# Weight copies on GpSimd, a longer last chunk and fewer closing passes in the setup of a fused conv, attention and mixture kernel

## The chip, the core and the metric

The kernel runs on one core of a Trainium2 chip. A core has five engines with a queue each: TensorE (PE in the profile), VectorE (DVE), ScalarE (ACT), GpSimd (POOL) and SyncE (SP), which here issues the DMAs. The metric is the device time of one launch in microseconds (us). It is 2541.94 us for the kernel before, the median of three runs.

## The reference

x has 128 images of 128 channels and 16 x 16 positions. Layer 0 normalises x by groups of four channels (32 groups) within each image, and puts that through a convolution block; layer 1 (two selective state-space scans and a mixture of eight experts on layer-normed tokens) takes most of the time and isn't touched by the change. Cut to what matters:

```python
def _gn(v, G=32, eps=1e-5):
    g = v.reshape(B_, G, C_ // G, H_, W_)
    m = jnp.mean(g, axis=(2, 3, 4), keepdims=True)
    s = jnp.var(g, axis=(2, 3, 4), keepdims=True)
    return ((g - m) / jnp.sqrt(s + eps)).reshape(v.shape)

def _bn(x, gamma, beta):
    m = jnp.mean(x, axis=(0, 2, 3), keepdims=True)
    v = jnp.var(x, axis=(0, 2, 3), keepdims=True)
    xhat = (x - m) * jax.lax.rsqrt(v + EPS)
    return xhat * gamma[None, :, None, None] + beta[None, :, None, None]

h = _act_quant(_bn(x, gamma1, beta1))          # clip to 0..1, 15 levels
wq1 = _weight_quant(w1) * pat1[None, None, :, :]
out = _conv3x3(h, wq1)
out = _act_quant(_bn(out, gamma2, beta2))
wq2 = _weight_quant(w2) * pat2[None, None, :, :]
out = _conv3x3(out, wq2)
return out + x

x = x + _L0_conv_ref(_gn(x), ...)
```

The batch norm needs the statistics of all images before one value of h can be made. Here it and the group norm are folded into one scale and one bias for each channel and image.

## The kernel before

**Stages.** The setup (about the first 77 us) reads x into 64 tiles `xr` of two images each, channels on the 128 partitions, and makes from it the scale `sc1` and the bias `bi1` (128 x 128: channel by image). `conv1` then quantises image pairs into padded tiles `hpad` and convolves them, with bfloat16 weights `wq1`; `conv2` follows, and then layer 1, whose steps stand in an order written out by hand.

**Statistics in chunks.** The images are cut in three chunks, `cuts = [0, 48, 112, 128]` for 128 images. VectorE takes the statistics of an image with `bn_stats` (L469). In the first two chunks every fourth image (b % 4 == 3, `by_scalar`) is ScalarE's instead: a pass that sums it (L464), a GpSimd pass over one column, `neg`, which makes the negative mean of it (L465), and a pass that sums the squares around that mean (L453). The square of an image stands behind the sum of the next one in ScalarE's queue, so one image lies between a `neg` and its use.

After a chunk's images its means and variances are made in 13 passes (L480 to L498), which stand on GpSimd for the first two chunks and on VectorE for the last; two of them go through TensorE, which averages over the four channels of a group (`gm_ps` L494, `gv_ps` L500), and ScalarE copies the one (L495) and takes the square root of the other (L502). VectorE takes the reciprocal (L472), and `normed` improves it by one Newton step and scales means and variances with it (L435 to L445), again on GpSimd for the first two chunks and on VectorE for the last. The reciprocal of the middle chunk is issued when the loop is at the last but one image:

```python
if b in (cuts[1] + 30, B - 2):
    with tc.issue_after(last.ins):
        nc.vector.reciprocal(ga[:, cuts[c - 1] : cuts[c]], ga[:, cuts[c - 1] : cuts[c]])
    normed(c - 1)
```

A scheduler puts the instructions of each engine into one queue, which is worked off in order; in VectorE's queue this reciprocal stands ahead of the statistics of image 127, and those ahead of the last chunk's passes.

**Closing the norm.** Over the 128 images VectorE makes the batch mean `bm` (L519, L520) and variance `bv` (L521 to L526), and GpSimd closes with six passes (L528 to L533): rs = (bv + EPS) ** -0.5, times 15 gamma (`g15`), sc1 = ga rs, bi1 = (shift - bm) rs + 15 beta (`b15`). A branch on the kind of the weights (L216 to L220) follows on every engine, and then `conv1`, which begins with ScalarE's passes over x with sc1 and bi1 (L547), like passes on GpSimd (L549), and VectorE's clipping into `hpad` (L183).

**Weights.** `conv_weights` quantises a convolution's weights (128 x 9 x 128 in float32), in steps that are set between the statistics. It makes three bfloat16 parts of them: the rounded weights (L160), the rounded rest (L174) and what is left after that (L176), with a subtraction on VectorE (L162) between the first two and one on GpSimd (L175) between the last two. The three copies are ScalarE's. It is called for w1 in the setup, and for w2 while `conv1` runs.

Of the kernel before, what the change touches and what calls it, by code (L numbers as in the profile page):

```python
# [11 lines left out]
ALU = mybir.AluOpType  # L12
# [4 lines left out]
EPS = 1e-5  # L17
# [17 lines left out]
def kernel(ctx: ExitStack, tc: tile.TileContext, a: dict):  # L35

    nc = tc.nc
    x_d, out_d = a["x"], a["out"]
    B = x_d.shape[0]
# [45 lines left out]
    mhalf = const.tile([P, 8], F32, name="mhalf")  # L85
# [25 lines left out]
    def row(name, ap):  # L111
        t = const.tile([P, ap.shape[0]], F32, name=name)
        nc.sync.dma_start(t, ap.partition_broadcast(P))
        return t
# [11 lines left out]

    CROSS, DIAGONAL = [1, 3, 4, 5, 7], [0, 2, 4, 6, 8]

    def conv_weights(parts, how, setup, psums, w, pat, taps, tag):


        def everywhere(n):

            mx_ps = psums.tile([P, P], F32, name=f"mx_ps_{tag}{n}", tag="mx_ps", bufs=1)
            nc.tensor.transpose(mx_ps, mx.to_broadcast([P, P]), ident)
            nc.vector.tensor_reduce(am, mx_ps, AX.X, ALU.max)

        t = setup.tile([P, 9, P], F32, name=f"t_{tag}", tag="t")
        nc.scalar.activation(t, w, AF.Tanh)
        yield  # L140
        mx = setup.tile([P, 1], F32, name=f"mx_{tag}", tag="mx")
        nc.vector.tensor_reduce(mx, t, AX.XY, ALU.max, apply_absolute_value=True)
        yield
        am = setup.tile([P, 1], F32, name=f"am_{tag}", tag="am")
        everywhere(0)
        yield
        nc.vector.tensor_scalar(am, am, 2.0, None, ALU.mult)
        rm = setup.tile([P, 1], F32, name=f"rm_{tag}", tag="rm")
        nc.vector.reciprocal(rm, am)
        nc.vector.tensor_scalar(t, t, rm, 0.5, ALU.mult, ALU.add)  # L150
        yield
        nc.vector.tensor_scalar(t, t, NLEV, MAGIC, ALU.mult, ALU.add)
        yield
        nc.vector.tensor_scalar(t, t, MAGIC, 2.0, ALU.subtract, ALU.mult)
        yield
        nc.vector.scalar_tensor_tensor(
            w, t, -NLEV, pat.unsqueeze(2).to_broadcast([P, 9, P]), ALU.add, ALU.mult
        )
        yield
        nc.scalar.copy(parts[:, :, 0, :], w)  # L160
        yield
        nc.vector.tensor_tensor(t, w, parts[:, :, 0, :], ALU.subtract)  # L162
        yield

        nc.vector.tensor_reduce(mx, t, AX.XY, ALU.max, apply_absolute_value=True)
        yield
        everywhere(1)
        yield
        nc.vector.tensor_scalar(am, am, 0.0, 2.0, ALU.not_equal, ALU.mult)
        for tap in range(9):  # L170
            if tap not in taps:
                nc.vector.scalar_tensor_tensor(am, pat[:, tap : tap + 1], 0.0, am, ALU.not_equal, ALU.max)
        nc.vector.tensor_copy(how, am)
        nc.scalar.copy(parts[:, :, 1, :], t)  # L174
        nc.gpsimd.tensor_tensor(w, t, parts[:, :, 1, :], ALU.subtract)  # L175
        nc.scalar.copy(parts[:, :, 2, :], w)  # L176

    def quantise(q, hp, nq):

# [64 lines left out]
    how1 = const.tile([P, 1], mybir.dt.int32, name="how1")  # L244
    how2 = const.tile([P, 1], mybir.dt.int32, name="how2")
    pat1, pat2 = row("pat1", a["L0_conv_pat1"]), row("pat2", a["L0_conv_pat2"])
# [90 lines left out]
    with tc.tile_pool(name="w1p", bufs=1) as w1p:  # L337

        sc1 = w1p.tile([P, B], F32, name="sc1")
        bi1 = w1p.tile([P, B], F32, name="bi1")  # L340
        wq1 = w1p.tile([P, 9, 3, P], BF16, name="wq1")
        o1st = res.tile([P, NP, 6], F32, name="o1st")
        with tc.tile_pool(name="setup1", bufs=1) as setup, tc.tile_pool(
# [45 lines left out]
            made = next(tables)  # L389
            w1 = w1p.tile([P, 9, P], F32, name="w1", tag="w")  # L390
            nc.sync.dma_start(w1, a["L0_conv_w1"])
            weights = conv_weights(wq1, how1, w1p, psa, w1, pat1, CROSS, "c1")
            with tc.issue_after(made.ins):
                next(weights)
            for _ in range(2):
# [15 lines left out]
            def tb(name):  # L411
                return setup.tile([P, B], F32, name=name)

            mean, var, dm, gm, dev, qv, ga, neg, shift = (
                tb(n) for n in ("mean", "var", "dm", "gm", "dev", "qv", "ga", "neg", "shift")
            )
            cuts = [0, 3 * B // 8, 7 * B // 8, B]
            half_ = setup.tile([P, B], F32, name="half_")
            b15 = setup.tile([P, 1], F32, name="b15")
            nc.vector.tensor_scalar(b15, bet1, NLEV, None, ALU.mult)  # L420
            g15 = setup.tile([P, 1], F32, name="g15")
# [96 lines left out]
            bm = setup.tile([P, 1], F32, name="bm")  # L518
# [4 lines left out]
            nc.vector.tensor_tensor(var, var, dev, ALU.add)  # L523
            bv = setup.tile([P, 1], F32, name="bv")
            nc.vector.tensor_reduce(bv, var, AX.X, ALU.add)
            nc.vector.tensor_scalar(bv, bv, 1.0 / B, None, ALU.mult)  # L526
            rs = setup.tile([P, 1], F32, name="rs")
            nc.gpsimd.tensor_scalar(rs, bv, EPS, None, ALU.add)  # L528
            nc.gpsimd.tensor_tensor(rs, rs, mhalf[:, 0:1], ALU.pow)
            nc.gpsimd.tensor_tensor(rs, rs, g15, ALU.mult)  # L530
            nc.gpsimd.tensor_scalar(sc1, ga, rs, None, ALU.mult)
            nc.gpsimd.tensor_scalar(bi1, shift, bm, rs, ALU.subtract, ALU.mult)
            nc.gpsimd.tensor_scalar(bi1, bi1, b15, None, ALU.add)  # L533


        def conv1(taps, nq):
            with tc.tile_pool(name="pb", bufs=3) as pb, tc.tile_pool(
                name="psb", bufs=4, space=PSUM
            ) as psb:
                weights = conv_weights(wq2, how2, w1p, psb, w2, pat2, DIAGONAL, "c2")  # L540

                def quantised(i):
# [659 lines left out]
    def part_f(i):  # L1202
# [84 lines left out]
    parts = {  # L1287
        "a": part_a, "c": part_c, "x": part_x, "bc": part_bc, "sx": part_sx, "z": part_z, "xt": part_xt, "g": part_g,
        "s": part_s, "b": part_b, "m": part_m, "y": part_y, "n": part_n, "r": part_r, "o": part_o, "e": part_e, "p": part_p,
        "f": part_f,  # L1290
    }
# [42 lines left out]
```

## Time and profile before

| | us |
|---|---|
| median of 3 runs (2541.1 to 2543.05) | 2541.94 |
| the profiled execution | 2543.71 |
| its span | 2542.0 |
| first matmul of the first convolution, into the span | 77.40 |
| VectorE busy, 57.50 to 64.60 | 0.00 |
| GpSimd busy, 57.50 to 64.60 | 4.46 |
| ScalarE busy, 57.50 to 64.60 | 2.90 |

The page of a profile has the busy time of each engine, and then the span in 40 slices of which each has one digit, the busy share in tenths. A line of a timeline has: start in the span, length (both us), engine, line of the kernel, operation, out<-in by the program's names, shapes as partitions x elements with the type, how often, and in square brackets how long the engine was idle before and what ended that. A line of the waits has: engine, what waited and its line, what it waited for and its line, then us in total, times, longest us.

### The profile page before, as it was taken

To read this page: it belongs to the slowest core of one execution; us is meant where nothing else is said; L and a number is where in the kernel's file an instruction comes from. 1 tells how busy PE (TensorE), PEld (TensorE's weight loads), DVE (VectorE), ACT (ScalarE), POOL (GpSimd) and SP (SyncE) were. 2 spreads that over 40 slices of the span, in tenths; PEclk is the share of its full clock that TensorE was granted. 3 is DMA by queue.
4 is the path that set the end of the run, shared out by engine and by line. 5 is a ranking of instruction groups with operands and counts; after the bars stand their busy time and mean duration, and the time that the engine had idled before them with its cause. 6 is when DMAs were issued, how large, how long until landed. Compare 5 with 4: busy or idle time off the path is not lost.

```text
span 2542.0 us, 49262 instructions
## 1 busy us (share of the span) xinstructions
PE 2412.9 (95%) x15936; PEld 1481.2 (58%) x15936; DVE 2239.5 (88%) x6094; ACT 2178.8 (86%) x4462; POOL 1639.8 (65%) x1733
## 2 busy tenths in 40 slices
PE   0888789999999999999999999999999999999997
PEld 0345456666666666666666666666666666666663
DVE  7886799999999999999999999999999999999883
ACT  7778699898889889888989888898988889898881
POOL 4677036666766666676666676666667666666676
PEclk9999899999999999999999999999999999999998
DMA  9368624444344444434434444443443444443333
GB/s 313 132 228 272 189 58 120 120 124 120 111 130 133 120 118 130 118 118 133 129 119 125 125 111 123 131 125 120 126 121 115 129 133 124 121 124 117 107 124 110
DMA packets 302166, 339.57 MB, mean 134 GB/s; under 512 B 56768, under 2 KB 226752, under 8 KB 301888
## 3 DMA queue, kind: packets, MB, share of 16 engines
q1 hardware_dynamic: 301888, 336.21, 43.4%
q8 instruction: 133, 2.18, 0.3%
q14 instruction: 145, 1.19, 0.2%
HBM read 262.72 MB, written 56.62 MB: 126 GB/s over the span
## 4 chain that ended last, share of the span: by engine, by line
PE 90%; DVE 3%; ACT 2%; issue 1%; DMA 1%; POOL 1%; SPq 0%; ACTq 0%; POOLq 0%; DVEq 0%
PE f_ps L1211 17%; PE x_ps L899 13%; PE y_ps L1034 10%; PE z_ps L942 9%; PE o_ps L1094 9%; PE sg L987 5%; PE xt_ps L954 4%; PE y_ps L1040 4%; PE g_ps L973 4%; PE cv L209 4%; PE n_ps L1067 1%; PE u_ps L1116 1%; PE f_ps L1206 1%; PE u_ps L772 1%; PE rt_ps L1123 1%; PE yt_ps L653 1%
## 5 line engine op out<-in xcount | busy, mean ns | idle before, releaser
L1199 POOL TENSOR_TENSOR gb<-gb,u2T 128x512 f32<-128x512 f32 x512 | 641.1, 1276 | 124.6 <-PE y_ps L1040 63.7
L917 DVE SCALAR_TENSOR_TENSOR xc<-x_ps,cw,xc 128x510 f32<-128x510 f32 (+2 forms) x768 | 570.9, 743 | 47.9 <-ACT xc L911 38.6
L1050 POOL TENSOR_TENSOR yg<-yg,z 128x512 f32<-128x512 f32 x256 | 325.8, 1278 | 349.1 <-DVE yg L1046 154.9
L1211 PE MATMUL f_ps<-gb,ew 128*128 128x512 f32 x1024 | 509.0, 601 | 7.2 <-POOL gb L1199 6.9
L899 PE MATMUL x_ps<-uT,wx 128*128 128x512 f32 x768 | 400.7, 603 | 9.5 <-ACT e L753 3.3
L753 ACT ACTIVATE e<-sg 128x512 f32<-128x512 f32 x512 | 299.3, 591 | 49.9 <-PE sg L987 44.4
L753 ACT ACTIVATE e<-e,ends 128x128 f32<-128x128 f32 x1024 | 325.0, 392 | 0.0
L1034 PE MATMUL y_ps<-e,xt 128*64 128x256 f32 x2048 | 317.7, 389 | 0.2 <-DVE yg L1046 0.2
L1015 DVE TENSOR_TENSOR e<-e,g_ps 128x1024 f32<-128x1024 f32 x256 | 311.2, 1216 | 5.6 <-ACT e L753 2.6
L917 DVE SCALAR_TENSOR_TENSOR bc<-x_ps,cw,bc 128x510 f32<-128x510 f32 (+2 forms) x384 | 286.5, 746 | 20.6 <-ACT bc L911 4.5
L1211 PEld LDWEIGHTS f_ps<-gb,ew 128*128 128x128 f32 x1024 | 180.5, 192 | 173.7 <-issue 135.4
L942 PE MATMUL z_ps<-uT,wz 128*128 128x512 f32 x512 | 272.2, 613 | 1.4 <-issue 0.8
L911 ACT ACTIVATE xc<-x_ps,cb,cw 128x512 f32<-128x512 f32 x256 | 199.0, 777 | 64.0 <-PE x_ps L899 57.1
L1094 PE MATMUL o_ps<-wo,yg 128*128 128x128 f32 x2048 | 251.4, 276 | 0.2 <-DVE e L1020 0.2
L1094 PEld LDWEIGHTS o_ps<-wo,yg 128*128 128x128 f32 x2048 | 240.5, 193 | 11.1 <-DVE g L1171 8.4
L1046 DVE SCALAR_TENSOR_TENSOR yg<-xc,dcol,y_ps 128x512 f32<-128x512 f32 x256 | 189.4, 740 | 50.5 <-PE y_ps L1040 47.1
L1082 POOL TENSOR_TENSOR rr<-rr,mhalf 128x8 f32<-128x8 f32 x64 | 110.0, 1718 | 161.7 <-DVE g L1173 82.5
L1040 PE MATMUL y_ps<-e,xt 128*64 128x128 f32 x2048 | 199.0, 273 | 0.0
L987 PE MATMUL sg<-rows,cols 128*128 128x256 bf16 x1024 | 192.1, 274 | 5.8 <-ACT e L753 2.9
L1040 PEld LDWEIGHTS y_ps<-e,xt 128*64 128x64 f32 x2048 | 147.0, 137 | 74.1 <-DVE e L1020 0.5
L1034 PEld LDWEIGHTS y_ps<-e,xt 128*64 128x64 f32 x2048 | 118.9, 136 | 100.9 <-issue 53.8
L209 PE MATMUL cv<-hpad,wq 128*128 128x512 bf16 x640 | 162.3, 398 | 12.8 <-DVE hpad L183 12.7
(283 smaller groups left out, 4810.2 us busy)
## 6 DMA issues: line engine op xcount, KB each, us to landing
gb<-gd SPq DMA_DIRECT2D x256, 512.0 KB
e<-cum SPq DMA_DIRECT2D x256, 256.0 KB
xr<-in_x SPq DMA_DIRECT2D x64, 256.0 KB
cc<-bc SPq DMA_DIRECT2D x128, 128.0 KB
out<-ob SPq DMA_DIRECT2D x64, 256.0 KB
y<-yt SPq DMA_DIRECT2D x60, 256.0 KB
yt<-y SPq DMA_DIRECT2D x60, 256.0 KB
o<-o SPq DMA_DIRECT2D x56, 256.0 KB
```

Of the source, the lines that this page charges most:

```text
L753: nc.scalar.activation(out, in_, func, **more)
L899: nc.tensor.matmul(ps, wx[d][:, n * P : (n + 1) * P], uTs[i], start=True, stop=True)
L917: nc.vector.scalar_tensor_tensor(acc[:, :, to], raw[:, :, of], cw[:, d, n, 3 - back : 4 - back], acc[:, :, to], ALU.mult, ALU.add,)
L942: nc.tensor.matmul(ps, wz[:, d, n * P : (n + 1) * P], uTs[i], start=True, stop=True)
L987: nc.tensor.matmul(sg[:, :, of], c_[:, k, d, s, half, :], r_[:, :, d, s, of], start=True, stop=True)
L1015: nc.vector.tensor_tensor(e0.rearrange("p h t l -> p h (t l)"), e0.rearrange("p h t l -> p h (t l)"), gps[i, d, k][:, 0:NT].unsqueeze(1).t ...
L1034: nc.tensor.matmul(y_ps[64 * q : 64 * q + 64, k, :], xt[:, 2 * k + s0, 64 * h : 64 * h + 64], e0[:, h].rearrange("p t l -> p (t l)"), star ...
L1040: nc.tensor.matmul(y_ps[64 * q : 64 * q + 64, k, s1 * P : (s1 + 1) * P], xt[:, 2 * k + s1, 64 * h : 64 * h + 64], e1[:, h, :], start=False ...
L1050: large(nc.gpsimd.tensor_tensor(yg, yg, zs[i, d][:, n, :], ALU.mult))
L1094: nc.tensor.matmul(o_ps[:, (2 * j + d) * P : (2 * j + d + 1) * P], ygs[i, d, n][:, t * P : (t + 1) * P], wo[d][:, n, :], start=(n == 0), s ...
L1199: large(nc.gpsimd.tensor_tensor(gb[:, e], gb[:, e], u2Ts[i], ALU.mult))
L1211: nc.tensor.matmul(f_ps, ew[:, e, :], gbs[i, e], start=False, stop=(e == NE - 1))
```

## The change

Three edits, all in the setup. `conv_weights` takes the function that makes its three bfloat16 copies as an argument, and for w1 that is GpSimd's `tensor_copy`; for w2 the copies stay with ScalarE. The cuts become 48, 104 and 128, so that the middle chunk has 56 images and the last 24, and ScalarE's share ends with image 103. And EPS is added by VectorE in the instruction that divides the variance, and GpSimd's six closing passes become four: shift = (shift - bm) g15, rs = bv ** -0.5, bi1 = shift rs + b15, sc1 = ga rs g15.

```diff
-    def conv_weights(parts, how, setup, psums, w, pat, taps, tag):
+    def conv_weights(parts, how, setup, psums, w, pat, taps, tag, cast=nc.scalar.copy):
...
-        nc.scalar.copy(parts[:, :, 0, :], w)
+        cast(parts[:, :, 0, :], w)
...
-        nc.scalar.copy(parts[:, :, 1, :], t)
+        cast(parts[:, :, 1, :], t)
         nc.gpsimd.tensor_tensor(w, t, parts[:, :, 1, :], ALU.subtract)
-        nc.scalar.copy(parts[:, :, 2, :], w)
+        cast(parts[:, :, 2, :], w)
...
-            weights = conv_weights(wq1, how1, w1p, psa, w1, pat1, CROSS, "c1")
+            weights = conv_weights(wq1, how1, w1p, psa, w1, pat1, CROSS, "c1", cast=nc.gpsimd.tensor_copy)
...
-            cuts = [0, 3 * B // 8, 7 * B // 8, B]
+            cuts = [0, 3 * B // 8, 13 * B // 16, B]
...
-            nc.vector.tensor_scalar(bv, bv, 1.0 / B, None, ALU.mult)
+            nc.vector.tensor_scalar(bv, bv, 1.0 / B, EPS, ALU.mult, ALU.add)
             rs = setup.tile([P, 1], F32, name="rs")
-            nc.gpsimd.tensor_scalar(rs, bv, EPS, None, ALU.add)
-            nc.gpsimd.tensor_tensor(rs, rs, mhalf[:, 0:1], ALU.pow)
-            nc.gpsimd.tensor_tensor(rs, rs, g15, ALU.mult)
-            nc.gpsimd.tensor_scalar(sc1, ga, rs, None, ALU.mult)
-            nc.gpsimd.tensor_scalar(bi1, shift, bm, rs, ALU.subtract, ALU.mult)
-            nc.gpsimd.tensor_scalar(bi1, bi1, b15, None, ALU.add)
+            nc.gpsimd.tensor_scalar(shift, shift, bm, g15, ALU.subtract, ALU.mult)
+            nc.gpsimd.tensor_tensor(rs, bv, mhalf[:, 0:1], ALU.pow)
+            nc.gpsimd.tensor_scalar(bi1, shift, rs, b15, ALU.mult, ALU.add)
+            nc.gpsimd.tensor_scalar(sc1, ga, rs, g15, ALU.mult, ALU.mult)
```

## The prediction

> **What bounds the kernel now.** The page comes first. It says TensorE is the bound of the whole, and slice 2 of 40 says where it isn't:
>
> ```profile
> PE 2412.9 (95%) x15936; PEld 1481.2 (58%) x15936; DVE 2239.5 (88%) x6094; ACT 2178.8 (86%) x4462; POOL 1639.8 (65%) x1733
> PE   0888789999999999999999999999999999999997
> ```
>
> A slice is 63.6 us. In the first one PE does nothing: it is the setup, in which x comes in, its statistics are taken and the first norm is closed. Everything after it follows in a fixed order behind the first convolution, so the change is worth what it takes off the moment when that convolution starts, 77.40 us into the span. The waits of the stretch 57 to 76 us and VectorE's timeline say what ends last there:
>
> ```profile
> DVE ga L472 <- ACT ga L502: 7.2, 1, 7.2
> ACT q L547 <- POOL bi L533: 7.1, 1, 7.1
> ```
> ```profile
> 51.81 5.64 DVE L469 BATCH_NORM_STATS2 bst<-xr 128x6 f32<-128x256 f32 x15 [0.33 <-DMA xr<-in_x]
> 64.61 0.55 DVE L472 RECIPROCAL ga<-ga 128x64 f32<-128x64 f32 x1 [7.17 <-ACT ga L502]
> 65.49 0.18 DVE L483 TENSOR_TENSOR mean<-bst 128x16 f32<-128x16 f32 x1
> 76.03 0.16 DVE L202 TENSOR_SCALAR less<-less_ps 128x1 f32<-128x1 f32 x1 [3.75 <-issue]
> ```
>
> VectorE has taken the statistics of all but one image by 57.45 us, when the last of x has come, and then stands 7.17 us: the reciprocal of the middle chunk is ahead of the last image in its queue and waits for that chunk's square root on ScalarE. So the last chunk starts at 65.45 and not at 57.9. Why the middle chunk is late is in ScalarE's timeline:
>
> ```profile
> 29.79 1.15 ACT L160 CAST wq<-w 128x1152 bf16<-128x1152 f32 x1 [3.21 <-DVE w L156]
> 38.49 1.14 ACT L174 CAST wq<-t_c 128x1152 bf16<-128x1152 f32 x1
> 42.11 1.15 ACT L176 CAST wq<-w 128x1152 bf16<-128x1152 f32 x1 [0.84 <-POOL w L175]
> 59.56 0.51 ACT L453 ACTIVATE junk<-xr,neg 128x256 f32<-128x256 f32 x1
> 64.27 0.31 ACT L502 ACTIVATE ga<-gv_ps,epsc 128x64 f32<-128x64 f32 x1 [2.44 <-PE gv_ps L500]
> ```
>
> ScalarE takes every fourth image of the first 112 (a sum, L464, and a square, L453, 1.235 us a pair, no gap from 48.4 on) and ends at 60.17, long after image 111 has come. In front of it stand the three weight copies, with two waits of 3.21 and 0.84 us. GpSimd's timeline has what the change touches there:
>
> ```profile
> 32.32 1.50 POOL L483 TENSOR_TENSOR mean<-bst 128x48 f32<-128x48 f32 x1
> 39.72 2.36 POOL L175 TENSOR_TENSOR w<-t_c,wq 128x1152 f32<-128x1152 f32 x1 [2.51 <-ACT wq L174]
> 72.36 0.23 POOL L528 TENSOR_SCALAR rs<-bv 128x1 f32<-128x1 f32 x1 [1.26 <-DVE bv L526]
> 72.67 0.58 POOL L529 TENSOR_TENSOR rs<-rs,mhalf 128x1 f32<-128x1 f32 x1
> 73.33 0.19 POOL L530 TENSOR_TENSOR rs<-rs,g 128x1 f32<-128x1 f32 x1
> 73.63 0.61 POOL L531 TENSOR_SCALAR sc<-ga,rs 128x128 f32<-128x128 f32 x1
> 74.23 0.81 POOL L532 TENSOR_SCALAR bi<-shift,bm,rs 128x128 f32<-128x128 f32 x1
> 75.14 0.61 POOL L533 TENSOR_SCALAR bi<-bi,b 128x128 f32<-128x128 f32 x1
> ```
>
> The last six are in series between VectorE's variance (72.28) and ScalarE's first pass over x (75.79).
>
> **What the Trainium skill says.** "Perfetto Trace Analysis", section "Tensor Engine Instruction": ScalarE, VectorE and GpSimd are strict FIFO. The trace agrees: ScalarE stood 3.21 us before L160 with image 47 landed. So a copy moved to GpSimd holds up what is queued behind it there. "SBUF — State Buffer", section "Who interferes with whom": a VectorE instruction with two SBUF inputs and a GpSimd instruction that reads SBUF exclude each other, whoever comes second waits for the other's end. The trace agrees: L483 on GpSimd took 1.50 us, against 0.38 for the wider one of the next chunk, and ended 0.19 us after VectorE's two-input L162 (32.29 to 33.63); VectorE's L172 over one column, issued at 40.33, ended at 42.10 with GpSimd's L175.
>
> **Part 1, copies on GpSimd.** No GpSimd copy stands in the trace of before. From below: the memset of 648 bfloat16 takes 0.637 us, so 0.83 ns a column and about 0.1 start, 1.06 us for 1152. The skill ("GPSIMD Engine Reference", section "4.1 Engine selection") calls one-input operations roughly line-rate, at 1.2 GHz an estimate of 0.96 and a 0.2 start, 1.16 us; no run here shows it. Between: the two-scalar pass of L549 takes 0.555 us for 256 columns where nothing disturbs it and the like pass L444 0.203 for 16, so 1.47 ns a column, 1.9 us for 1152. From above: the one-operation passes (0.614 for 128 columns, 0.214 for one) cost 3.15 ns a column, 3.8 us. I take 1.2, since a copy computes nothing.
>
> The order of the built program shows where they stand. ScalarE only loses the three copies and two images. On GpSimd the first copy is before neg of image 47, the second before L175, the third between neg of 59 and of 63, and the eight first passes of the first chunk's Newton step now stand before neg of 79. Behind a copy waits neg (L465), and for it ScalarE's square. With the durations above:
> - first copy 29.83 (w is ready at 29.75) to 31.03, neg of 47 to 31.26, then the 13 passes L480 to L498. They took 31.72 to 36.84 with 1.3 us of the lock in it; it stays, since L162 still comes at 32.29: 31.26 to 36.24.
> - neg of 51 and 55 to 36.70, second copy to 37.90, L175 (2.36) to 40.32, neg of 59 to 40.55: ScalarE's square of 59 at 40.61 instead of 43.17.
> - third copy to 41.75, neg of 63 to 41.98, its square at 42.04 instead of 44.40.
> - then 1.235 us an image, but the square of 79 waits for the Newton step (44.74 to 47.31) and comes at 47.60. Six pairs on, the square of 103 ends at 55.07.
>
> That is 60.17 - 55.07 = 5.1 us, of which the two images are 2.47. A tenth more for a copy costs 0.3 us, since three stand in series.
>
> **Part 2, chunks of 48, 56 and 24.** Beside the two images: the 13 passes over 56 columns instead of 64 save 0.03 us each, 0.4 us, so the last chunk starts 5.5 us earlier, at 59.95. That is still after x's last image, at 57.45, so VectorE's two more statistics (0.34 us each, by 57.9) are hidden; 2 us are left before the DMA is the bound. VectorE's 20-odd passes over 24 columns instead of 16 cost 0.009 us each (0.17 at 16, 0.29 at 128), +0.2 us. The middle chunk's Newton step on GpSimd starts from the same reciprocal as before and so keeps its distance of 3 us from VectorE's sum L519.
>
> **Part 3, four closing passes.** L528 and L530 go, EPS rides on L526 for nothing. After the variance: 0.08 wait, 0.58 power, 0.1, then bi1 (multiply and add, as L549, 0.39 for 128 columns), 0.1, then sc1 (two products, between L531's 0.61 and L532's 0.81: 0.7), 0.04: 2.0 us instead of 3.51, 1.5 less. But two things eat it. VectorE comes back from the branch at 76.03, 3.75 us after its variance whatever GpSimd does, and the first padded image, which ScalarE let start at 76.91, could then start at 76.1 at best: 0.8 of the 1.5. And the pass over shift (0.81, as L532) now runs on GpSimd from the moment L445 has ended (71.09 in before's times), held behind L522 to 71.37, so to 72.2; VectorE's two-input L523, due at 71.48, must wait for it, +0.7. Sum of the tail with the 24 columns: -0.8 + 0.7 + 0.2 = +0.1. If L523 doesn't wait and ScalarE's earlier start counts in full, it is -1.3.
>
> **Sum.** -5.5 + 0.1 = -5.4 us. The profiled execution took 2543.71 us, its span and 1.71 around it, so 2538.3 by its own time; it lies 1.77 above the median of 2541.94, and by the median the forecast is 2536.5. Later stages I let move as a block: SP's queue isn't altered, its weight loads are issued by 83.3 us and the first store of o1 would come at about 86; w2, issued at 53.8, is used at about 79.
>
> **Rivals.** 0.2% is 5.1 us here, about what a measurement of this kernel can tell from no change.
> - The tail pays: 5.5 + 1.3 = 6.8, 2535.1. For it: the lock needs L528 to start in a gap of 0.1 us. Against: L172 and L483 show that it bites.
> - The copies run at the pace of the q passes (1.9 us): the same steps give 62.0 for the last chunk, 3.4 us gained, 2538.6 with the tail. For it: that pass is the nearest one-input row over a long tile. Against: it computes, a copy doesn't.
> - Slower: GpSimd's queue takes ScalarE's place as the bound, at the third copy and L465 behind it. At 3.8 us a copy the same steps put the square of 63 some 4.5 us later than before and the last chunk at 67.8: 2.4 us lost, 2544.4. It decides from 3.0 us a copy, where the last chunk starts at 65.4. For it: the one-operation passes do run that slowly. Against: those are arithmetic passes.
> - The gain is lost later, 2542: something after the first convolution's start would have to wait for what hasn't moved. Against: PE is busy for 77.6 of the 80.4 us that follow 77.40, and the transfers of that stage end early.
>
> **Chances.** Forecast 0.50 (0.37 of it beyond 5.1 us, as it lies on the line), tail pays 0.20, q pace 0.20 (0.02 beyond), slower 0.06 (half of it beyond 5.1 us the other way, if a copy is slower still), lost later 0.04. So faster 0.59, slower 0.03, same 0.38. The range goes from the tail's case with copies of 1.06 us and 0.9 us of scatter (2533.8) to copies of 2.4 us, whose last chunk starts at 63.6 (2540.3); it leaves out the slower and lost cases.
>
> **What would show it.** Copies on GpSimd of 1.2 us; ScalarE's last square near 55; VectorE's reciprocal L472 near 59; L523 held until the shift pass ends; the first convolution's first matmul near 72. It is wrong if a copy takes 2 us or more, or if the first matmul moves and the end doesn't.

## The result, and the profile after

| | before | after |
|---|---|---|
| median, us (11 runs each) | 2543.05 (2540.63 to 2548.52) | 2536.57 (2534.36 to 2538.47) |
| ratio, 95% interval | | 0.9973 [0.9963, 0.9982] |
| the profiled execution | 2543.71 | 2536.24 |
| its span | 2542.0 | 2534.5 |

The changed kernel is 6.5 us faster by the medians (4.6 to 9.4 by the interval); 5.4 were forecast. That the forecast of 2536.5 lies so near the median of 2536.57 is partly luck, since the kernel before ran 1.1 us longer beside it than in the three runs that the forecast started from. The comparison that counts is 5.4 against 6.5, and it has to be made stage by stage.

The page of the changed kernel, its busy times and TensorE's row of the 40 slices:

```profile
PE 2415.3 (95%) x15936; PEld 1480.5 (58%) x15936; DVE 2241.5 (88%) x6096; ACT 2174.2 (86%) x4451; POOL 1641.9 (65%) x1732
PE   0889889999999999999999999999999999999997
```

TensorE is busy for 2.4 us longer than before and the kernel is shorter nevertheless: what went is idle time, 6.3 us of it ahead of the first convolution, which the digits are too coarse to show. The waits of the stretch 50 to 76 us show it:

```profile
ACT q L545 <- POOL sc L531: 5.4, 1, 5.4
...
DVE less L202 <- issue: 3.7, 1, 3.7
...
DVE ga L472 <- ACT ga L502: 1.4, 1, 1.4
```

VectorE's wait for the middle chunk's square root was 7.2 us and is 1.4. VectorE's timeline of the changed kernel, the lines that answer to those of before:

```profile
58.85 0.50 DVE L472 RECIPROCAL ga<-ga 128x56 f32<-128x56 f32 x1 [1.40 <-ACT ga L502]
59.67 0.20 DVE L483 TENSOR_TENSOR mean<-bst 128x24 f32<-128x24 f32 x1
...
65.97 0.35 DVE L523 TENSOR_TENSOR var<-var,dev 128x128 f32<-128x128 f32 x1
...
66.68 0.15 DVE L526 TENSOR_SCALAR bv<-bv 128x1 f32<-128x1 f32 x1
70.54 0.16 DVE L202 TENSOR_SCALAR less<-less_ps 128x1 f32<-128x1 f32 x1 [3.70 <-issue]
70.61 0.76 DVE L183 TENSOR_SCALAR hpad<-q 128x512 uint8<-128x512 f32 x2
```

The last chunk starts at 59.67, before at 65.49. The variance is ready at 66.83, VectorE is back from the branch at 70.54, and the first padded image follows at once; before, it stood 0.73 us more until ScalarE had made its input. GpSimd's timeline of the changed kernel has the three copies and the four closing passes:

```profile
29.82 1.14 POOL L160 CAST wq<-w 128x1152 bf16<-128x1152 f32 x1 [3.57 <-DVE w L156]
...
36.59 1.14 POOL L174 CAST wq<-t_c 128x1152 bf16<-128x1152 f32 x1
...
40.31 1.14 POOL L176 CAST wq<-w 128x1152 bf16<-128x1152 f32 x1
...
65.70 0.85 POOL L528 TENSOR_SCALAR shift<-shift,bm,g 128x128 f32<-128x128 f32 x1
66.92 0.58 POOL L529 TENSOR_TENSOR rs<-bv,mhalf 128x1 f32<-128x1 f32 x1 [0.37 <-DVE bv L526]
67.61 0.45 POOL L530 TENSOR_SCALAR bi<-shift,rs,b 128x128 f32<-128x128 f32 x1
68.04 0.45 POOL L531 TENSOR_SCALAR sc<-ga,rs,g 128x128 f32<-128x128 f32 x1
```

And ScalarE's timeline of the changed kernel: the square of image 59, the last square (image 103), and the middle chunk's root.

```profile
40.39 0.51 ACT L453 ACTIVATE junk<-xr,neg 128x256 f32<-128x256 f32 x1 [0.59 <-POOL neg L465]
...
53.99 0.51 ACT L453 ACTIVATE junk<-xr,neg 128x256 f32<-128x256 f32 x1
...
58.51 0.31 ACT L502 ACTIVATE ga<-gv_ps,epsc 128x56 f32<-128x56 f32 x1 [2.34 <-PE gv_ps L500]
```

The square of 59 waits 0.59 us behind the second copy and the subtraction on GpSimd, which is what the copies cost there, and the last square starts at 53.99 instead of 59.56.

How far the gain reaches, as starts in us into the span; the marks are those that the runs below are compared by:

| | before | after | gain |
|---|---|---|---|
| last chunk's first pass (L483) | 65.49 | 59.67 | 5.82 |
| variance (L526) | 72.13 | 66.68 | 5.45 |
| first padded image (L183) | 76.91 | 70.61 | 6.30 |
| first matmul of the first convolution | 77.40 | 71.09 | 6.31 |
| first matmul of the second convolution | 164.56 | 158.95 | 5.61 |
| first `dt_ps` matmul of layer 1 | 280.76 | 275.04 | 5.72 |

So 5.8 us come at the last chunk, the tail adds 0.5, the first convolution gives 0.7 back, and layer 1 starts 5.7 us earlier. The remaining 1.8 of the span's 7.5 appear inside layer 1, where two executions of one kernel can differ by more (last lines of the section on the first convolution).

### The profile page after: what moved, and what is told of

Same layout as the page of the kernel before. It is cut to its first block, busy times and chain, and to the rows that moved or that the text cites. A ratio compares the mean times of both kernels' runs of the same rounds, so it can differ in the third digit from the quotient of the medians.

```text
span 2534.5 us, 49248 instructions
## 1 busy us (share of the span) xinstructions
PE 2415.3 (95%) x15936; PEld 1480.5 (58%) x15936; DVE 2241.5 (88%) x6096; ACT 2174.2 (86%) x4451; POOL 1641.9 (65%) x1732
## 4 chain that ended last, share of the span: by engine, by line
PE 89%; DVE 4%; DMA 3%; ACT 2%; POOL 1%; issue 1%; SPq 0%; DVEq 0%; POOLq 0%; ACTq 0%
PE f_ps L1209 17%; PE x_ps L897 13%; PE y_ps L1032 10%; PE z_ps L940 9%; PE o_ps L1092 9%; PE sg L985 5%; PE xt_ps L952 4%; PE y_ps L1038 4%; PE g_ps L971 4%; PE cv L209 4%; DMA xr<-in_x 2%; PE n_ps L1065 1%; PE f_ps L1204 1%; PE u_ps L1114 1%; PE u_ps L770 1%
## 5 line engine op out<-in xcount | busy, mean ns | idle before, releaser
L1032 PEld LDWEIGHTS y_ps<-e,xt 128*64 128x64 f32 x2048 | 118.9, 136 | 101.0 <-issue 54.0
```

Source lines behind the costliest of these rows:

```text
L1032: nc.tensor.matmul(y_ps[64 * q : 64 * q + 64, k, :], xt[:, 2 * k + s0, 64 * h : 64 * h + 64], e0[:, h].rearrange("p t l -> p (t l)"), star ...
```

## The experiments

The theory was that of the prediction: parts 1 and 2 both shorten ScalarE's queue and so the wait at L472, and the tail is worth little because VectorE comes back from the branch late. The rivals were its own (the tail counts in full, copies at the q passes' pace, GpSimd's queue is the new bound, the gain is lost later), and one more: one part alone carries the gain. Every run is compared with the kernel before on its own chip; the medians of different rows come from several chips, so the ratios and the starts are to be compared, not the medians.

| run | last chunk | first matmul | second conv. | median, us | ratio [95%] |
|---|---|---|---|---|---|
| e1_copies | 62.36 | 74.31 | 162.40 | 2540.71 | 0.9985 [0.9978, 0.9992] |
| e2_cut | 62.82 | 75.05 | 163.14 | 2542.45 | 0.9994 [0.9985, 1.0002] |
| e3_closing | 65.50 | 76.48 | 164.25 | 2543.74 | 0.9997 [0.9989, 1.0005] |
| e4_twice | 60.58 | 72.08 | 159.55 | 2539.15 | 0.9980 [0.9971, 0.9989] |
| e5_cut96 | 58.01 | 69.62 | 157.54 | 2537.32 | 0.9970 [0.9959, 0.9980] |
| e6_sc_twice | 59.61 | 70.73 | 159.15 | 2539.11 | 0.9979 [0.9973, 0.9986] |
| e7_scalar_var | 60.19 | 71.27 | 158.39 | 2538.01 | 0.9975 [0.9966, 0.9983] |
| e9_mult | 65.48 | 76.92 | 164.05 | 2542.86 | 0.9997 [0.9989, 1.0006] |
| e9_muladd | 59.73 | 71.25 | 159.06 | 2536.41, one run | |
| e8_warm | 59.63 | 71.07 | 157.56 | 2535.61 | 0.9971 [0.9962, 0.9980] |
| e10_best | 58.19 | 69.60 | 156.74 | 2535.14 | 0.9965 [0.9951, 0.9978] |
| e11_again | 59.69 | 70.86 | 158.88 | 2540.13, one run | |

### One part at a time

Each of the first three is the changed kernel with two of its three parts undone. What the first undoes is the cut and the closing:

```diff
-            cuts = [0, 3 * B // 8, 13 * B // 16, B]
+            cuts = [0, 3 * B // 8, 7 * B // 8, B]
...
-            nc.gpsimd.tensor_scalar(shift, shift, bm, g15, ALU.subtract, ALU.mult)
...
+            nc.gpsimd.tensor_scalar(rs, bv, EPS, None, ALU.add)
```

> Only the copies go to GpSimd; cuts and closing passes are those of the kernel before. Queue theory (the last chunk waits for GpSimd's and ScalarE's queues, and every edit acts through them): with copies of 1.14 us, as measured in the changed kernel, the steps of the prediction put ScalarE's last square at 57.4 us instead of 60.2 and the last chunk's first pass at 62.7 instead of 65.5; first matmul of the first convolution 2.8 us earlier than before, at 74.6. Rival (GpSimd gives back what ScalarE is spared, since the squares wait for the one-column passes behind the copies, and the whole gain is the cut's): last chunk at 65.5 and no gain.

The second undoes the copies (and the closing, as above), so that the cut stands alone:

```diff
-            weights = conv_weights(wq1, how1, w1p, psa, w1, pat1, CROSS, "c1", cast=nc.gpsimd.tensor_copy)
+            weights = conv_weights(wq1, how1, w1p, psa, w1, pat1, CROSS, "c1")
```

> Only the cuts change (48, 104, 128). Queue theory: two images fewer on ScalarE, 2.47 us, last square at 57.7, last chunk's first pass at 63.0; the longer last chunk gives back 0.2, first matmul about 2.3 us earlier, at 75.1. Rival (the cut is the whole gain): last chunk near 59.7 and the first matmul near 71.6.

VectorE's timeline of the kernel with the copies alone, and then of the one with the cut alone:

```profile
61.49 0.55 DVE L472 RECIPROCAL ga<-ga 128x64 f32<-128x64 f32 x1 [4.08 <-ACT ga L502]
62.36 0.18 DVE L483 TENSOR_TENSOR mean<-bst 128x16 f32<-128x16 f32 x1
```
```profile
61.99 0.50 DVE L472 RECIPROCAL ga<-ga 128x56 f32<-128x56 f32 x1 [4.32 <-ACT ga L502]
62.82 0.20 DVE L483 TENSOR_TENSOR mean<-bst 128x24 f32<-128x24 f32 x1
```

The reader is to see the wait in brackets: 7.17 us before, some 4 with either part, 1.40 with both. The last chunk comes 3.13 us earlier with the copies and 2.67 with the cut; their sum, 5.80, is what the changed kernel shows, 5.82. Neither part carries the gain alone and neither hides the other: both shorten the same queue.

The third keeps the closing alone: it undoes the copies, as just shown, and the cut, by the first two lines of the diff ahead of that.

> Only the closing passes change (four, and EPS on VectorE). The prediction's tail: ScalarE's first pass over x 1.5 us earlier after the variance than before, but the first padded image bound by VectorE's return from the branch, so first matmul 0.8 us earlier than before at most, near 76.6; and if GpSimd's pass over shift held VectorE's L523 it would be 0.1 us. Rival (the closing passes count in full): 1.5 to 1.8 us earlier, 75.7.

Its VectorE timeline:

```profile
71.50 0.35 DVE L523 TENSOR_TENSOR var<-var,dev 128x128 f32<-128x128 f32 x1
...
75.93 0.16 DVE L202 TENSOR_SCALAR less<-less_ps 128x1 f32<-128x1 f32 x1 [3.56 <-issue]
76.00 0.76 DVE L183 TENSOR_SCALAR hpad<-q 128x512 uint8<-128x512 f32 x2
```

The first padded image comes 0.91 us earlier than before (76.91) and stands directly behind VectorE's return: of ScalarE's 1.7 us (75.79 to 74.07) 0.9 count. And L523 takes 0.35 us where it took 0.29, while GpSimd's pass over shift runs from 71.23 to 72.09 across it: it isn't held. First matmuls add up as well: 3.09, 2.35 and 0.92 make 6.36, against 6.31 in the changed kernel. Such agreement is better than the traces allow one to expect, since VectorE's return from the branch alone takes between 3.4 and 3.8 us over the traces.

### What a copy may cost

The first try made each of the three copies twice:

```diff
-        cast(parts[:, :, 0, :], w)
+        for _ in range(1 if cast == nc.scalar.copy else 2):
+            cast(parts[:, :, 0, :], w)
```

> The changed kernel with each of w1's three copies made twice in a row on GpSimd, the same values, so 2.28 us of GpSimd's queue for each. Queue theory: three in series and the one-column passes behind them, 3 us for each us added: last chunk's first pass at 63.3 instead of 59.7, first matmul near 74.6, 3.5 us later than in the changed kernel. Rival (GpSimd has idle time there which hides them): last chunk at 59.7 as in the changed kernel, since GpSimd is busy for a third of that stretch.

GpSimd's timeline of that kernel at the first pair:

```profile
29.75 1.14 POOL L161 CAST wq<-w 128x1152 bf16<-128x1152 f32 x1 [3.57 <-DVE w L156]
30.86 0.21 POOL L468 TENSOR_SCALAR neg<-bst 128x1 f32<-128x1 f32 x1
31.02 1.14 POOL L161 CAST wq<-w 128x1152 bf16<-128x1152 f32 x1
```

The last chunk came only 0.91 us later, far less than expected. The reason is the middle line: the scheduler set an image's `neg` between the two copies, so ScalarE's square didn't wait for the second one. Six copies in another order are not three copies of twice the length, so this run doesn't answer the question.

The next two leave the order of every queue as in the changed kernel and write the copy as another instruction with the same values, a product with 1.0, and the product followed by adding 0.0:

```diff
-            weights = conv_weights(wq1, how1, w1p, psa, w1, pat1, CROSS, "c1", cast=nc.gpsimd.tensor_copy)
+            weights = conv_weights(wq1, how1, w1p, psa, w1, pat1, CROSS, "c1", cast=lambda o, i: nc.gpsimd.tensor_scalar(o, i, 1.0, None, ALU.mult))
```

> The changed kernel with w1's three copies made by GpSimd's one-operation pass (times 1.0), the same values, in the same places of every queue. It is the prediction's slower rival at its price: 3.15 ns a column, 3.8 us each. Queue theory (3 us for each us of a copy, order unchanged): last chunk's first pass at 67.5 to 67.8, 8 us later than in the changed kernel and 2.2 later than in the kernel before, first matmul near 79; time 8 us above the changed kernel's. Rival (as the doubled copies seemed to say, GpSimd's idle time hides most of it): last chunk below 62.

```diff
+            ... cast=lambda o, i: nc.gpsimd.tensor_scalar(o, i, 1.0, 0.0, ALU.mult, ALU.add))
```

> The changed kernel with each of the three copies written as a two-operation pass (times 1.0, plus 0.0), which gives the same values: the pace of the q passes, 1.47 ns a column, that one rival gave to the copies. That rival's price is 1.9 us for 1152 columns; with 2.88 us of delay for each us of a copy, as the one-operation pass showed, the last chunk then starts at 59.67 + 0.76 x 2.88 = 61.9. If a copy's length counted only once, or not at all, it would start at 60.4 or 59.7.

GpSimd's and VectorE's timelines of the kernel with the product:

```profile
29.64 3.18 POOL L392 TENSOR_SCALAR wq<-w 128x1152 bf16<-128x1152 f32 x1 [3.58 <-DVE w L156]
```
```profile
64.66 0.50 DVE L472 RECIPROCAL ga<-ga 128x56 f32<-128x56 f32 x1 [4.87 <-ACT ga L502]
...
65.48 0.20 DVE L483 TENSOR_TENSOR mean<-bst 128x24 f32<-128x24 f32 x1
```

At 3.16 us a copy (mean of the three; 3.8 had been expected) the last chunk starts at 65.48, where it started before the change: all that parts 1 and 2 won is gone, and the ratio is 0.9997 [0.9989, 1.0006]. Each us of a copy costs (65.48 - 59.67) / (3.16 - 1.14) = 2.9 us, near the 3 of "three stand in series". That is the prediction's slower rival, measured at the point where it begins to decide; it had put that point at 3.0 us.

With the product and sum, GpSimd's timeline says:

```profile
29.82 1.15 POOL L392 TENSOR_SCALAR wq<-w 128x1152 bf16<-128x1152 f32 x1 [3.58 <-DVE w L156]
```

1.15 us and not the expected 1.9: this pass is as fast as the copy, and the last chunk starts at 59.73 as in the changed kernel. So the run adds no third point to the slope, but it removes the rival that gave a copy "the pace of the q passes". That price had been drawn through two unlike passes, L444 over 16 columns with constants and L549 over 256 with factors from a column each. L444 alone, 0.203 us for 16 columns and 0.243 for 64 in the trace of before, gives 0.83 ns a column, and so an estimate of 1.15 us for 1152: the trace of before held the right price for this form.

### How far the cut goes

```diff
-            cuts = [0, 3 * B // 8, 13 * B // 16, B]
+            cuts = [0, 3 * B // 8, 3 * B // 4, B]
```

> The changed kernel with cuts 48, 96, 128: ScalarE is spared two more images, VectorE takes them. Queue theory: in the changed kernel VectorE still stood 1.40 us before the middle chunk's reciprocal; two images are 2.47 us, so that wait goes, the transfers of x end last and the last chunk's first pass is at 57.9 to 58.3 instead of 59.7; 0.2 us given back over 32 columns; first matmul 1.2 to 1.6 us earlier than 71.1, at 69.6. Rival (VectorE itself becomes late with two more statistics, as it keeps pace with the transfers only just): last chunk no earlier than 59.

VectorE's timeline of that kernel:

```profile
57.26 0.43 DVE L472 RECIPROCAL ga<-ga 128x48 f32<-128x48 f32 x1
...
58.01 0.21 DVE L483 TENSOR_TENSOR mean<-bst 128x32 f32<-128x32 f32 x1
```

No wait for ScalarE stands before the reciprocal any more: VectorE is bound by x's arrival, where the prediction had 2 us left. The last chunk moves 1.66 us, the first matmul 1.47 (69.62), the second convolution 1.41. In the total time it can't be told from the changed kernel (0.9970 [0.9959, 0.9980]).

### What bounds the tail

Two runs on the stretch between variance and first padded image. One makes the last closing pass twice, so that ScalarE starts later:

```diff
-            nc.gpsimd.tensor_scalar(sc1, ga, rs, g15, ALU.mult, ALU.mult)
+            for _ in range(2):
+                nc.gpsimd.tensor_scalar(sc1, ga, rs, g15, ALU.mult, ALU.mult)
```

> The changed kernel with its last closing pass (sc1, 0.45 us) made twice. The prediction's reading of the tail (the first padded image waits for VectorE's return from the branch, not for GpSimd): ScalarE's first pass over x 0.45 us later after the variance, 2.15 instead of 1.70 us, and the first padded image still 3.8 us after it, so the first matmul doesn't move against the variance. Rival (the closing passes are on the path): the first matmul 0.45 us later after the variance.

The other takes VectorE out earlier: the two sums of the variance become ScalarE passes with an accumulator, and GpSimd adds them, so that VectorE ends with the mean.

```diff
-            nc.vector.tensor_tensor(dev, dev, dev, ALU.mult)
-            nc.vector.tensor_tensor(var, var, dev, ALU.add)
...
-            nc.vector.tensor_reduce(bv, var, AX.X, ALU.add)
+            nc.scalar.activation(junk[:, :B], var, AF.Copy, accum_out=sums2[:, 0:1])
+            nc.scalar.activation(junk[:, :B], dev, AF.Square, bias=nbm, accum_out=sums2[:, 1:2])
...
+            nc.gpsimd.tensor_tensor(bv, sums2[:, 0:1], sums2[:, 1:2], ALU.add)
```

> The changed kernel with the batch variance taken by ScalarE (one pass that sums the variances, one that sums the squares around the batch mean, with accumulators) and two one-column passes on GpSimd in place of VectorE's five passes, so VectorE goes to the branch right after the batch mean. If VectorE's return from the branch is what the first padded image waits for, it comes 1.5 us earlier (the five passes end 1.6 us after the mean) unless the closing passes are then last: mean to first pass over x near 3.2 us as before, and 1.1 us to its end, so first padded image about 4.3 us after the mean instead of 5.4; first matmul near 70.0. Rival (the branch takes as long as it needs to be done by about 70, whatever its start[...]): first matmul at 71.1.

VectorE's timelines, first with the doubled pass, then with the variance on ScalarE:

```profile
70.18 0.16 DVE L202 TENSOR_SCALAR less<-less_ps 128x1 f32<-128x1 f32 x1 [3.40 <-issue]
70.26 0.42 DVE L183 TENSOR_SCALAR hpad<-q 128x512 uint8<-128x512 f32 x1
```
```profile
69.51 0.16 DVE L202 TENSOR_SCALAR less<-less_ps 128x1 f32<-128x1 f32 x1 [3.58 <-issue]
70.79 0.43 DVE L183 TENSOR_SCALAR hpad<-q 128x512 uint8<-128x512 f32 x1 [1.12 <-ACT q L547]
```

With the doubled pass ScalarE starts 2.25 us after the variance instead of 1.70, and the first padded image is no later after the variance: it still follows VectorE's return. So the closing passes have slack, and VectorE's way through the branch sets the end. In the changed kernel the slack is some 0.9 us: ScalarE starts at 68.53, needs about 1.1 us for the two passes of the first pair, and VectorE comes at 70.54.

The second run takes VectorE's way out: VectorE is back 3.8 us after the mean instead of 5.3, and the padded image now waits 1.12 us for ScalarE. It comes 5.06 us after the mean, where 5.39 was the changed kernel's figure and 4.3 was expected: of 1.5 us, 0.3 count. But what holds ScalarE isn't the closing passes, as GpSimd's and ScalarE's timelines of that kernel show:

```profile
68.59 0.45 POOL L533 TENSOR_SCALAR sc<-ga,rs,g 128x128 f32<-128x128 f32 x1
...
66.45 0.18 ACT L525 ACTIVATION_READ_ACCUMULATOR junk<-dev,nbm 128x1 f32 x1
69.66 3.06 ACT L547 ACTIVATE q<-xr,bi,sc 128x256 f32<-128x256 f32 x6 [3.03 <-DMA cb<-in_L_attn_fwd_conv_b]
```

sc1 is ready at 69.04, and ScalarE starts at 69.66. The edit gave ScalarE work up to 66.63. The trace has its compare-and-branch (L219) ending at 66.72 and its next instruction at 69.60: its own return has become the last one. (The DMA in the brackets loads a tile that this pass doesn't read.) Behind sc1, as in the changed kernel, it would have started some 0.6 us earlier, an estimate from these lines, so that 0.9 of the 1.5 us would have counted, the slack found above. The first matmul, at 71.27, lies near the rival's 71.1, but the rival's reason fails: VectorE did return earlier, 3.58 us after its last pass, and the whole tail began 0.5 us late in this execution (last chunk at 60.19). Shortening one of the chains stops at the next.

### Where the first convolution gives 0.7 us back

The windows of TensorE's `cv` matmuls, in steps of 2 us from the first one, in the kernel before and then in the changed one. The first figure is the stretch, then its length, then PE's busy time with the number of matmuls in it (one that crosses a border counts on both sides), then VectorE's and ScalarE's, the granted clock, the DMA share and GB/s:

```profile
77.00:79.00 2.00, 1.60 (x4) 0.00 (x0) 0.00 (x0) 1.00 0.15 18
79.00:81.00 2.00, 2.00 (x6) 0.00 (x0) 0.69 (x1) 1.00 0.12 6
81.00:83.00 2.00, 2.00 (x10) 0.00 (x0) 1.06 (x2) 1.00 0.09 2
```
```profile
71.00:73.00 2.00, 1.91 (x5) 0.00 (x0) 0.00 (x0) 1.00 0.08 9
73.00:75.00 2.00, 2.00 (x6) 0.00 (x0) 0.69 (x1) 1.00 0.59 137
75.00:77.00 2.00, 2.00 (x8) 0.00 (x0) 0.69 (x1) 1.00 0.48 81
77.00:79.00 2.00, 2.00 (x10) 0.00 (x0) 1.37 (x2) 1.00 0.14 18
```

PE counts as busy from the first matmul on, and the granted clock is printed as 1.00; only the count shows that the first matmuls take twice the time. They start 0.43 us apart and then mostly 0.22 to 0.24. That lasts 3.4 us before, and 5.0 after (the expectation below has 5.9). At half pace half of the time is lost, so the 1.5 us more cost some 0.8, an estimate, against 0.7 given back. It fits that TensorE's busy time from one convolution's first matmul to the other's grows from 77.86 to 78.56 us, and its idle time stays 9.30. Two causes were open, the array's own start and padded images that come late. The next run puts nine matmuls that nobody reads into TensorE's wait ahead of the first padded image:

```diff
+            spare = psums.tile([P, 4, P], F32, name="spare", tag="cv")
+            for n in range(9):
+                nc.tensor.matmul(spare, wq[:, 0, 0, :], wq[:, 0:4, 0, :], start=True, stop=True)
```

> The changed kernel, with nine more matmuls of 128x512 over the first convolution's own weights, behind less_ps, whose output nobody reads. They stand where TensorE waits 4.4 us for the first padded image (66.73 to 71.09 in the changed kernel), so the first real matmul stays near 71.1. Theory: the changed kernel gave back 0.70 us of its gain because TensorE runs at about 0.4 us a matmul for 15 matmuls (5.9 us) after the start, against 8 matmuls (3.4 us) before, and this slow pace depends on how long TensorE has been busy: the spare matmuls then take it, the real ones run at 0.23 us from the first, and conv2's first matmul comes 1 to 2.5 us earlier, at 156.5 to 158, where the later supply of padded images lets it. Rival: the first fifteen are slow because padded images come late; then their pace stays at 0.39 us, and conv2's first matmul stays at 158.9. In the total time at most 0.1%, beside the scatter of 1 to 2 us.

TensorE's timeline and its windows in that kernel:

```profile
66.76 3.62 PE L205 MATMUL spare<-wq 128*128 128x512 bf16 x9
71.07 17.65 PE L213 MATMUL cv<-hpad,wq 128*128 128x512 bf16 x75 [0.69 <-DVE hpad L183]
```
```profile
71.00:73.00 2.00, 1.93 (x9) 0.00 (x0) 0.56 (x1) 1.00 0.10 11
73.00:75.00 2.00, 2.00 (x10) 0.00 (x0) 0.79 (x2) 1.00 0.60 140
```

The same first matmul, and full pace from there: nine in the first stretch instead of five. The second convolution starts at 157.56, 1.39 us earlier than in the changed kernel. Late padded images are out as a cause; the half pace is TensorE's start after its idle time, and the spare matmuls take it.

What sets its length is in the traces' own records of the clock, each with a start, a length and a granted share of 0.50 or 1.00. The first record of a trace, a 1.00, starts where the full pace starts: at 80.84 us before, 3.44 after the first matmul, and at 76.06 after, 4.97 after it. Nothing is recorded ahead of it, so the 1.00 in the windows above stands for no record. Later the clock drops and returns, in the changed kernel first from 154.57 to 164.81 us, where 0.50 is granted. In all fourteen traces every such record starts a whole number of steps of 3.413 us behind the first one, to the end of the kernel (here 23 and 26 steps). So the clock changes only on a grid, and where the grid lies against the kernel differs from one trace to the next. The full pace came with the first step that closed a nearly busy interval: one in which TensorE had been busy for 2.96 of the 3.41 us counted (cut at 96), one with 2.61 didn't (doubled pass).

The Trainium skill bears on this: "TensorE: Matmul & The Clock Gate", section "Part 1: The HAM clock gate", says that the array runs at half rate until it has been busy for a window of about 3.4 us, that this window runs free of the kernel's start, and that the number of slow matmuls differs from run to run. The traces agree with the factor of two and with the free-running window. The length isn't one window of 3.4 us, though, but anything from 3.0 to 6.0, and the first convolution's length follows it:

| half pace, us | runs | first convolution, us |
|---|---|---|
| 3.2 to 3.4 | product, before, variance on ScalarE | 87.1 to 87.2 |
| 3.8 | copies made twice | 87.5 |
| 4.5 to 5.0 | closing alone, product and sum, after | 87.8 to 87.9 |
| 5.2 to 5.5 | copies alone, second trace of after (below), cut alone | 88.0 to 88.1 |
| 6.0 | doubled pass | 88.4 |

The cut at 96 is the exception (3.0 us and 87.9): there TensorE stands idle 0.5 us longer than in the runs of the table, for a reason that no run follows up.

Whether the length belongs to the kernel or to the execution was asked of a second trace of the unaltered changed kernel:

> The changed kernel once more, unaltered, for a second trace of it. The question is whether the length of TensorE's half pace at the start of the first convolution belongs to the kernel or to the execution. If to the kernel, the trace shows 3, 4, 4, 4, 3, 6 matmuls in the first six us again and 87.9 us from the first convolution's first matmul to the second one's. If to the execution (a window that isn't tied to the kernel's start), the count is another one, anything from the 3, 4, 4, 6 to the 3, 4, 4, 4, 3, 4 that the runs so far show, and the length follows it, 87.1 where full pace comes by the fifth us and 87.8 to 88.4 where it comes later. Everything up to the first matmul should be as before, within 0.2 us: last chunk at 59.7, first matmul at 71.1.

The half pace lasted 5.3 us there, and the first convolution 158.88 - 70.86 = 88.0 us, against 87.9 in the first trace and 87.2 before. The two traces of this kernel happen to agree, but the table says what they agree in: where the first matmul fell between two steps of the clock's grid. Kernels that start earlier and later got the short and the long half pace (69.62: 3.0, 70.73: 6.0, 71.27: 3.4, 75.05: 5.5, 76.92: 3.2). So the 0.7 us is what the traced executions of before and after differ by in that; that the change costs it in every execution is not shown, with one trace of before and two of after.

The same trace answers another question. From the second convolution's first matmul to layer 1's first `dt_ps` it took 118.9 us, and the first trace of the same kernel 116.1. Over all runs this stretch lies between 113.4 and 119.6 us (116.2 before). So one kernel's executions differ there by 2.8 us, as much as the effects in question: edits that move the start by 1 or 2 us can be lost in it. The clock goes with it here too: the five traces whose clock stays at 1.00 between 170 and 270 us are the shortest (113.4 to 115.6), the nine with 3.4 or 6.8 us at half clock there take 115.8 to 119.6. Which of the two brings the other is not shown.

### Both together

The cut at 96 with the nine spare matmuls:

> The two that moved the start together: the middle chunk cut at image 96 and the nine spare matmuls. If they add, the first matmul comes at 69.6 as with the cut alone and conv2's first matmul at 155.5 to 157.5 (the cut alone 157.54, the changed kernel 158.95). Rival: with the cut alone the slow pace had been short already, so the spare matmuls bring nothing on top and conv2's first matmul stays at 157.5. Time against the kernel before: 0.9965 of it, 8.5 us less, if all of it reaches the end; 0.9973, as for the changed kernel, if the scatter of the later stages hides it.

The first matmul comes at 69.60 and the second convolution at 156.74, 0.80 us before the cut alone and 2.21 before the changed kernel, so the two add in part. With the cut alone the half pace was short already (3.0 us), and here 1.7 us of it are left: the spare matmuls began at 65.44, but the next step of the grid with a busy interval behind it came only at 71.27. The median, 2535.14, is the lowest of all, and the ratio 0.9965 [0.9951, 0.9978] overlaps that of the changed kernel, 0.9973 [0.9963, 0.9982]. It beats the kernel before; that it beats the changed one is not shown.

## Why the prediction was right, and where it was not

**Part 1, right.** A copy was taken at 1.2 us and measures 1.14. Of the stated prices, the 1.16 worked out from the skill's "GPSIMD Engine Reference", section "4.1 Engine selection", came nearest; that one-input operations run at that rate held for the copy, and not for the product with a constant (3.16 us). The steps hold in their order: the square of 59 was put at 40.61 and stands at 40.39, that of 79 at 47.60 and stands at 47.09, and the last ends at 54.60 instead of 55.07. Most of that half us is there when the Newton step ahead of the square of 79 begins, at 44.28 and not at 44.74; the shorter copies are worth about 0.2 of it by the slope of 2.9. The 36.24 given for the end of the 13 passes doesn't follow from their 5.12 us behind 31.26, which make 36.38; they ended at 36.28, and nothing hung on it.

**Part 2, right.** "The last chunk starts 5.5 us earlier, at 59.95": 59.67, and the two parts add. That x's last image isn't the bound yet, with 2 us left, is shown by the cut at 96, which uses 1.66 of them. The 24 columns were put at 0.2 and cost 0.3: from the last chunk's first pass to the variance it takes 6.64 us before and 6.95 with the cut alone.

**Part 3, the term "+0.7" failed.** The step said that VectorE's L523 must wait until the pass over shift ends. It ran through inside that pass, 65.97 to 66.32 against 65.70 to 66.55, and took 0.06 us more. Nor was the pass held behind L522 (65.58 to 65.87), as the step had it. The 0.8 for VectorE's return was right (0.9 with the closing alone), and so was the reason, that the return comes 3.75 us after the variance "whatever GpSimd does": 3.71 measured, and 3.40 with the doubled pass, where GpSimd works longer; over the traces it lies between 3.4 and 3.8. In the changed kernel the tail is therefore worth -0.5 and not +0.1. ScalarE's first pass came 1.70 us after the variance, 2.0 were expected, because the pass with two products takes 0.45 and not 0.7; nothing hung on that.

**"Later stages I let move as a block", off by 0.7 us in the traces.** The first matmul moved by 6.31, the second convolution by 5.61. The prediction had looked for transfers that haven't moved, and TensorE's idle time in the first convolution is indeed unchanged. What it left out was TensorE's own start, whose length is set by the clock's grid in each execution and not, as far as the runs show, by the change.

**The sum.** -5.4 was forecast, and the stages say -5.8 - 0.5 + 0.7 = -5.6 up to the second convolution and -5.7 at layer 1. An error of 0.3 in parts 1 and 2, one of 0.6 in the tail and one of 0.7 the other way nearly cancelled; the three have separate causes, so that this is luck. The rest up to the 6.5 of the medians is less than what executions of one kernel differ by inside layer 1.

**The rivals.** Copies at the q passes' pace: refuted by their time. Slower from 3.0 us a copy: not what happened, but the mechanism is real and its point was right, while its price was not: a one-operation pass over 1152 columns takes 3.16 us and not 3.8. Gain lost later: 0.7 of 6.3 in the traces, not all. The tail pays: its first half came true, L523 doesn't wait; its second didn't, since of ScalarE's earlier start 0.9 us count.

## What to carry to other kernels

Work moved from a late engine to an idle one is worth its time only as long as the instruction that replaces it is short: three in series multiply its price by three, so find out what the very form of instruction costs on the new engine, since a copy and a product on GpSimd differ by a factor of 2.8 here, and a price drawn through two different forms holds for neither. When a stage ends in two chains that lie a us apart, the slack of the second is the most that shortening the first can bring. And where an engine waits anyway ahead of a dense stretch, look whether its first instructions run at full pace, by counting them in windows; a busy share doesn't show it. How long they don't can differ by 3 us between executions, so two single traces don't tell what a change costs there.

## What the runs showed of the hardware

- GpSimd over 1152 columns, float32 to bfloat16: a copy takes 1.14 us, a product with a constant 3.16, and a product and a sum with constants 1.15. Here two operations are faster than one.
- The skill's "SBUF — State Buffer", section "Who interferes with whom", has a two-input VectorE instruction and a GpSimd instruction that reads SBUF exclude each other. It held for a one-input pass of GpSimd in the changed kernel, L484 (1.43 us instead of some 0.3, beginning while VectorE's two-input L162 ran), and for the third copy: VectorE's L172 over one column began at 41.03 and ended at 41.46, with the copy (40.31 to 41.45). It did not hold for L528, a GpSimd pass with two factors from a column each, across which L523 ran in 0.35 us instead of 0.29 in the changed kernel, in the closing alone and in the product run, while L528 itself took 0.85 against 0.81 where VectorE ran nothing beside it (variance on ScalarE). Why not is open.
- TensorE after idle time places matmuls of 128x512 at 0.43 us instead of 0.22 to 0.24, for 3.0 to 6.0 us. The full pace begins with the first clock record of the trace, and all later changes of the clock lie on a grid of 3.413 us behind it; the grid's place against the kernel differs from trace to trace.
- A branch on a loaded value costs an engine some 3 us. From the end of its compare-and-branch (L219 in the changed kernel) to its next instruction it takes VectorE, ScalarE, GpSimd and SyncE 2.45 to 3.42 us over all traces, and TensorE's own record of that instruction lasts 3.3 to 4.0.
